# First tokens of a gate-and-mixture kernel: two load queues, means ahead of scales, and another order of the first norms

## The chip, the cores and the metric

The kernel runs on one core of one Trainium2 chip. Its time is the device time of that core in microseconds (us): the median of four runs, 842.18 us (841.93 to 842.66). Beside these there is one profiled execution, whose trace is read below.

## The reference, cut to what matters

Tokens x are 4096 rows of 1024 numbers. Each row is normed, the normed rows feed a gate and a three-layer expert path, and the result is added to x.

```python
xn = (x - mean(x, -1)) / sqrt(var(x, -1) + 1e-5)
g  = sigmoid(xn @ gate_w.T + gate_b)          # product "g"
u_g = xn * g                                  # then a recurrence over tokens and its mean
h  = silu(xn @ w1.T)                          # product "u"
h  = silu(h @ w3.T)                           # product "m"
h  = h @ w2.T
route = top2(softmax(xn @ wr.T))              # expert numbers 0..7 and their gates
out[expert] += gate * h                       # rows 0..7 of the expert output
result = x + recurrence(u_g) * silu(out)
```

Only rows 0 to 7 of the expert output are ever written, so the large products are summed over tokens by expert, and all other rows of the result are rows of x.

## The kernel before, in words

**Tiling.** The tokens are worked off in four super-blocks (`sb`) of 1024. In each the normed tokens stand transposed, as four blocks `xn[sb, I, J]` of 128 partitions x 2048 numbers: I is the half of the tokens, J the half of the channels. A block has four parts of 128x512; `part(block, a)` takes the two that hold token quarter (I, a), as four slices of 256 tokens. The products u (w1), g (gate_w, in super-block 0 alone) and m (w3) are made by seven products of half-size matrices, twice nested: each `Half` is one of the outer seven, and takes seven or eight steps of `small`, four matmuls of 256 columns each. Sums of weight blocks (`fresh_sums`) and of token blocks (`left_sums`) that this needs are made by GpSimd (POOL) into 128x512 tiles `q`. Product 1 of u and g is "plain": eight steps without such sums.

**The first norm.** In super-block 0, mean and variance come from the tokens as they stand in memory. `load_x0` brings 256 rows; `stats0(I, a, ...)` runs on VectorE (DVE): statistics (`bn`), aggregation (`mv`), a root on ScalarE (`sd`), a correction step (`scales`), and two pairs of diagonals (`dg`) with the means and with the scales. Two matmuls with a matrix of ones, `lag` places later in the order, spread them as rows of 256 over all partitions, in a PSUM tile `bc`. `norm0(I, a, J)` then subtracts the mean row and multiplies by the scale row. The quarters (0,0) and (0,1) have their rows in `bc_00` and in `acc`, (1,0) in `bc_10` and (1,1) in `bc_11`. `bc_11` lies in the pool `ps_sm`, which has one bank; ahead of it, `idle` lay there. Sixteen matmuls into `idle` run at the very start, with operands made on the chip.

**What sets the order.** A list `todo` holds steps with a place; the loop at the end runs the steps of the halves by place and, ahead of each, what is due. The order in which instructions are recorded is the order on each engine's queue; an instruction waits for what it reads and for those who still use what it overwrites. Product 1 of u has the places 0 to 14, that of g 3 to 17, product 2 of u begins at 16, and its left-hand sums at 10. The norms have places: (0,1) at 4.6, and block `xn[0,0,1]` at 4.8 and 5. The first sum of `left_sums` for product 2 reads two parts of `xn[0,0,1]`.

**Loads.** All are issued by SyncE (SP), in the order recorded; a load also waits for the landing of the eighth before it. First come the 256 rows in four quarters, the transposed block in quarters between the two halves of w1's first block, the rows of (0,1), gate_w's first block, and the rest of the transposed block.

Lines that matter: at the end of the kernel `idle`, `load_x0(0, 0, 4)`, `first_weights(...)` and the `at(...)` calls of `stats0` and `norm0`.

Of the kernel before, what the change touches and what calls it, by code (L numbers as in the profile page):

```python
# [10 lines left out]
F32 = mybir.dt.float32  # L11
I32 = mybir.dt.int32
U32 = mybir.dt.uint32
AF = mybir.ActivationFunctionType
ALU = mybir.AluOpType
AX = mybir.AxisListType
P = 128
Q = 256
# [4 lines left out]
def kernel(  # L23
# [50 lines left out]
    H = 512  # L74
# [48 lines left out]
                self.home.append(self.tile)  # L123

    NB, NQ = 20, 18
    IDLE = 16
    blocks = deque(
        const.tile([P, 4, 2 * Q], F32, tag=f"b{i}", name=f"b{i}") for i in range(NB)
    )
# [4 lines left out]
    def block(uses=1):  # L134
        return Held(blocks, uses)

    def quarter(uses=1):
        return Held(quarters, uses)
# [5 lines left out]
    pool.memset(ones, 1.0)  # L144
    eps = const.tile([P, 1], F32, tag="eps", name="eps")
    pool.memset(eps, EPS)

    root = const.tile([P, 1], F32, tag="root", name="root")
    act.activation(root, eps, AF.Sqrt)
# [26 lines left out]
    def at(place, f, *args):  # L176

        seq[0] += 1
        heapq.heappush(todo, (place, seq[0], f, args))
# [42 lines left out]
    def scales(o, v, sd, w):  # L222

        r0 = sp.tile([P, w], F32, tag=f"r{w}", name="r0")
        dve.reciprocal(r0, sd)
        e = sp.tile([P, w], F32, tag=f"e{w}", name="e")
        dve.scalar_tensor_tensor(e, r0, -0.5, r0, ALU.mult, ALU.mult)
        dve.tensor_mul(e, e, v)
        dve.scalar_tensor_tensor(o, e, 1.5, r0, ALU.add, ALU.mult)

    def part(t, a):
        return t[:, 2 * a : 2 * a + 2, :].rearrange("p b (k n) -> p (b k) n", n=Q)
# [3 lines left out]
    def stats0(I, a, xb, lag):  # L236

        mv = sp.tile([P, 2, 2], F32, tag="mv", name=f"mv_{I}{a}")
        for tt in range(2):
            xt = xb[:, 2 * tt : 2 * tt + 2, :]  # L240
            bn = sp.tile([P, 2, nc.vector.BN_STATS_DIM], F32, tag=f"bn{tt}", name=f"bn_{I}{a}{tt}")
            for n in range(2):
                dve.bn_stats(bn[:, n, :], xt[:, n, :])
            dve.bn_aggr(mv[:, tt, :], bn)
        xb.drop()
        sd = sp.tile([P, 2], F32, tag="sd2", name=f"sd_{I}{a}")
        act.activation(sd, mv[:, :, 1], AF.Sqrt, bias=eps)
        dg = quarter()

        def diagonals(s, w):  # L250
            for tt in range(2):
                dve.tensor_scalar(
                    dg[:, (2 * s + tt) * P : (2 * s + tt + 1) * P],
                    ident,
                    w[:, tt : tt + 1],
                    None,
                    ALU.mult,
                )

        diagonals(0, mv[:, :, 0])  # L260
        v = sp.tile([P, 2], F32, tag="v2", name=f"v_{I}{a}")
        dve.tensor_scalar(v, mv[:, :, 1], EPS, None, ALU.add)
        rs = sp.tile([P, 2], F32, tag="rs", name=f"rs_{I}{a}")
        scales(rs, v, sd, 2)
        diagonals(1, rs)
        if (I, a) == (1, 1):
            bc = ps_sm.tile([P, 2, Q], F32, tag="sm", name="bc_11")
        elif (I, a) == (1, 0):
            bc = ps_y.tile([P, 2, Q], F32, tag="Y", name="bc_10")
        elif a == 1:  # L270
            bc = acc.rearrange("p (s n) -> p s n", s=2)
        else:
            bc = ps_acc.tile([P, 2, Q], F32, tag="rows", name="bc_00")
        yield lag
        for s in range(2):
            pe.matmul(
                bc[:, s, :],
                ones,
                dg[:, s * Q : (s + 1) * Q],
                start=True,  # L280
                stop=True,
                skip_group_check=True,
            )
        dg.drop()
        bc0[I, a] = bc

    def norm0(I, a, J, parts=1):
        p = part(xn[0, I, J], a)
        bc = bc0[I, a]
        w = 4 // parts  # L290
        for h in range(0, 4, w):
            for s, op in ((0, ALU.subtract), (1, ALU.mult)):
                row = bc[:, s : s + 1, :].to_broadcast([P, w, Q])
                dve.tensor_tensor(p[:, h : h + w, :], p[:, h : h + w, :], row, op)

    def stats(sb, bcs):

# [158 lines left out]
    T_OF = ((1, 0, None), (3, None, 0), (3, 1, None), (2, None, 1))  # L456
    T_AT = (1, 2, 4, 6)

    def load_w(name, KN, uses, before=()):
        t = block(uses)  # L460
        if not before:
            sync.dma_start(t.tile, weights[name][KN])
        for b, f in enumerate(before):
            f()
            sync.dma_start(t[:, b::2, :], weights[name][KN][:, b::2, :])
        return t

    def t_sum(o, t, s, j):
# [87 lines left out]
        sync.dma_start(o.tile, kept[{"u": "w1", "m": "w3"}[kind], i, j])  # L556
        op_ts[kind, sb, i, j] = o

    def first_weights(kind, name, before=()):

        keep = name == "w1"

        def S(i):
            return start[kind, 0, i]

        b = {}

        def load(key, KN, uses, *before):
            b[key] = load_w(name, KN, uses, *before)

        def one():

            op_t[kind, 0, 1] = b[1]

        def two():
            op_t[kind, 0, 2] = b[2]

        def five():
            yield from sub(pool, b[5], b[5], b[1])
            b[1].drop()  # L580
            op_t[kind, 0, 5] = b[5]
            if keep:
                keep_block(name, 5, b[5])

        def six():
            yield from with_bank(b[6], b[6], b[5])
            b[5].drop()
            op_t[kind, 0, 6] = b[6]
            if keep:
                keep_block(name, 6, b[6])  # L590

        def seven():

            yield from sub(pool, b[7], b[6], b[7])
            b[6].drop()
            op_t[kind, 0, 7] = b[7]
            if keep:
                keep_block(name, 7, b[7])

        def four():  # L600
            yield from with_bank(b[4], b[4], b[6])
            b[6].drop()
            op_t[kind, 0, 4] = b[4]
            if keep:
                keep_block(name, 4, b[4])

        def three():
            op_t[kind, 0, 3] = b[3]

        off = 0 if kind == "u" else 1  # L610
        load(1, (0, 0), 2, before)
        one()
        at(-20 + off, lambda: load(2, (1, 0), 2))
        at(-19, two)
        at(-12 + off, lambda: load(5, (0, 1), 3 + keep))
        at(S(5) - 13, five)
        at(2 + off, lambda: load(6, (1, 1), 4 + keep))
        at(S(6) - 16, six)
        at(S(6) - 3 + off, lambda: load(7, (0, 0), 2 + keep))
        at(S(7) - 12, seven)  # L620
        at(S(6) + 8 + off, lambda: load(4, (1, 0), 2 + keep))
        at(S(4) - 14, four)
        at(S(3) - 14, lambda: load(3, (1, 1), 2))
        at(S(3) - 13, three)
        for i in order["u"][1:]:
            if kind == "g" and i in PLAIN_G:
                at(S(i) - 4, lambda i=i: op_t[kind, 0, i].drop())
                continue
            at(
                S(i) + 2 - (11 if i == 2 else 6),  # L630
                lambda i=i: fresh_sums(kind, i, op_t[kind, 0, i], keep),
            )
# [407 lines left out]
    def load_x0(I, a, n=2):  # L1040
        xb = block()
        row = I * H + a * 2 * P
        w = 2 * D // n
        for h in range(n):
            t, c = h * w // D, h * w % D
            sync.dma_start(
                xb.tile.rearrange("p h d -> p (h d)")[:, h * w : (h + 1) * w],
                x[row + t * P : row + (t + 1) * P, c : c + w],
            )
        x0[I, a] = xb  # L1050
# [12 lines left out]
    USES = {(0, 0): 4, (0, 1): 3, (1, 0): 3, (1, 1): 3}  # L1063
    G = {(0, 0): 2, (0, 1): 2, (1, 0): 1, (1, 1): 2}


    idle = ps_sm.tile([P, P], F32, tag="sm", name="idle")
    for _ in range(IDLE):
        pe.matmul(idle, ones, ident, start=True, stop=True, skip_group_check=True)
    load_x0(0, 0, 4)  # L1070
    first = block(USES[0, 0] + G[0, 0])
    xn[0, 0, 0] = first
    first_weights(
        "u",
        "w1",
        [
            lambda b=b: sync.dma_start(first[:, b, :], xT[0, 0, 0, :, b, :])
            for b in range(2)
        ],
    )  # L1080
    load_x0(0, 1)
    first_weights("g", "gw")
    sync.dma_start(first[:, 2:4, :], xT[0, 0, 0, :, 2:4, :])
    at(-27, load_x0, 1, 0)
    at(-26, load_x0, 1, 1)
    at(-25, load_xn, 0, 0, 1, USES[0, 1] + G[0, 1])
    at(-16, load_xn, 0, 1, 0, USES[1, 0] + G[1, 0])
    at(-15, load_xn, 0, 1, 1, USES[1, 1] + G[1, 1])
    at(-10, lambda: stats0(0, 0, x0[0, 0], 0))
    at(-9, norm0, 0, 0, 0, 2)  # L1090
    at(-8, lambda: stats0(0, 1, x0[0, 1], 12.5))
    at(-7, lambda: stats0(1, 0, x0[1, 0], 14))
    at(4.6, norm0, 0, 1, 0)
    at(4.7, lambda: stats0(1, 1, x0[1, 1], 7.5))
    at(4.8, norm0, 0, 0, 1)
    at(5, norm0, 0, 1, 1)
    at(8, norm0, 1, 0, 0)
    at(11, norm0, 1, 0, 1)
    at(15, norm0, 1, 1, 0)
    at(18, norm0, 1, 1, 1)  # L1100
    at(26, consts)
    for IJ in HB:
        at(0, lambda IJ=IJ: left.__setitem__(("u", 0, IJ), xn[(0,) + IJ]))
# [276 lines left out]
```

## Time and profile before

| | us |
|---|---|
| median of four runs | 842.18 (841.93 to 842.66) |
| the profiled execution | 843.08 |
| its span, first to last instruction | 841.3 |
| TensorE matmuls (PE) | 829.0, 99% of the span |
| VectorE (DVE) | 546.3, 65% |
| GpSimd (POOL) | 490.2, 58% |
| ScalarE (ACT) | 243.2, 29% |
| mean granted clock of TensorE | 0.997 of full |

The share of an engine is an average over the whole span. The change touches the first 45 us of it, so the rows of those microseconds count. In a row of the timeline stand the start, the duration, the engine, the operation, output and inputs with their shapes, the number of instructions merged (x), and in brackets the idle time ahead of it with what ended it. The profile counts two records to one matmul of 32-bit numbers. All rows have the line of the helper that records them (L89), so they are told apart by the tiles: `b` is a block, `q` a quarter, `bc` and `acc` hold spread rows, `X_u` is a PSUM tile of product u.

### The profile page before, as it was taken

Reading aid. Unit: us, or ns where it says so; the run is one execution under the profiler, and the core shown is the slowest. Engines: PE = TensorE matmul, PEld = TensorE weight load, DVE = VectorE, ACT = ScalarE, POOL = GpSimd, SP = SyncE. Lnnn points to the kernel's source line nnn. Section 1 sums busy time; section 2 is a strip of 40 time slices with the busy share of each in tenths; the row PEclk is TensorE's granted clock in tenths of the full one; section 3 lists DMA queues with packets and bytes.
Section 4 is the critical chain, followed back from the end, with each engine's and each line's share of the span. In section 5 each row is a group of like instructions: output and inputs, shape, how many; then the busy total and the mean of one; then the engine's idle time right before and its main releaser. Section 6 shows DMA issues by size and latency. Waiting matters only on the chain.

```text
span 841.3 us, 11288 instructions
## 1 busy us (share of the span) xinstructions
PE 829.0 (99%) x4119; PEld 701.6 (83%) x4119; DVE 546.3 (65%) x890; ACT 243.2 (29%) x391; POOL 490.2 (58%) x377
## 2 busy tenths in 40 slices
PE   7999999999999999999999999999999999999997
PEld 6887888888888868888888778888888688888884
DVE  6965699888579427675897225675993246645643
ACT  0214205866121207343012226531122021220112
POOL 0379888785878758546346753753548444474400
PEclk9999999999999999999999999999999999999999
DMA  9935428622995979728966757649774546545700
GB/s 339 422 146 221 155 89 311 226 113 70 396 395 190 317 269 364 287 87 321 407 222 245 269 179 271 237 164 400 284 265 167 184 164 236 201 160 198 282 13 2
DMA packets 55679, 194.97 MB, mean 232 GB/s; under 512 B 6356, under 2 KB 9668, under 8 KB 43592
## 3 DMA queue, kind: packets, MB, share of 16 engines
q1 hardware_dynamic: 55592, 194.24, 62.3%
q8 instruction: 33, 0.54, 0.3%
q14 instruction: 22, 0.18, 0.1%
q10 hardware_dynamic: 32, 0.02, 0.0%
HBM read 171.10 MB, written 39.87 MB: 251 GB/s over the span
## 4 chain that ended last, share of the span: by engine, by line
PE 92%; DMA 3%; DVE 2%; POOL 1%; issue 1%; SPq 0%; ACT 0%; POOLq 0%; DVEq 0%
PE X_u L89 23%; PE X_m L89 20%; PE Z_u L89 12%; PE Z_m L89 11%; PE Y_u L89 6%; PE X_g L89 6%; PE Y_m L89 5%; PE Z_g L89 4%; PE acc L89 2%; PE plT L89 2%; DMA b<-in_w 2%; DVE b L89 1%; DMA w<-q 1%; POOL q L89 1%; PE Y_g L89 1%
## 5 line engine op out<-in xcount | busy, mean ns | idle before, releaser
L89 POOL TENSOR_TENSOR q<-b 128x512 f32<-128x512 f32 x144 | 198.2, 1389 | 230.4 <-DVE b L89 52.7
L89 ACT ACTIVATE b<-b 128x512 f32<-128x512 f32 (+1 forms) x152 | 105.0, 696 | 315.8 <-DVE b L89 311.4
L89 DVE TENSOR_TENSOR b<-b,b 128x512 f32<-128x512 f32 x160 | 155.3, 988 | 2.9
L89 POOL TENSOR_TENSOR q<-b,q 128x512 f32<-128x512 f32 x91 | 130.0, 1432 | 8.8 <-issue 6.7
L89 POOL TENSOR_TENSOR b<-b,b 128x512 f32<-128x512 f32 x72 | 94.8, 1342 | 35.9 <-PE X_u L89 26.4
L89 DVE TENSOR_TENSOR b<-X_u,b 128x512 f32<-128x512 f32 x87 | 59.9, 689 | 72.4 <-PE X_u L89 71.5
L89 PE MATMUL X_u<-q,q 128*128 128x256 f32 x432 | 103.0, 381 | 0.0
L89 DVE TENSOR_TENSOR b<-X_m,b 128x512 f32<-128x512 f32 x84 | 57.4, 687 | 63.7 <-PE X_m L89 63.4
L89 PE MATMUL X_m<-q,q 128*128 128x256 f32 x416 | 98.5, 380 | 0.0
L89 PEld LDWEIGHTS X_u<-q,q 128*128 128x128 f32 x432 | 81.3, 190 | 14.9 <-POOL q L89 1.7
L89 POOL TENSOR_TENSOR q<-q,b 128x512 f32<-128x512 f32 x53 | 71.9, 1357 | 34.5 <-PE X_u L89 28.9
L89 PEld LDWEIGHTS X_m<-q,q 128*128 128x128 f32 x416 | 78.8, 190 | 11.8 <-issue 0.8
L89 DVE TENSOR_TENSOR b<-b,bc 128x1024 f32<-128x1024 f32 (+1 forms) x62 | 72.8, 1178 | 6.2 <-ACT bc L89 5.2
L89 PE MATMUL X_m<-b,b 128*128 128x256 f32 x272 | 63.8, 380 | 0.9 <-POOL b L89 0.9
L89 PE MATMUL X_u<-b,b 128*128 128x256 f32 x248 | 60.4, 388 | 2.8 <-DVE b L89 2.5
L89 PEld LDWEIGHTS X_m<-b,b 128*128 128x128 f32 x272 | 51.3, 190 | 8.6 <-POOL b L89 1.2
L89 PEld LDWEIGHTS X_u<-b,b 128*128 128x128 f32 x248 | 48.0, 195 | 10.7 <-DVE b L89 3.3
L89 PE MATMUL X_u<-b,q 128*128 128x256 f32 x216 | 51.3, 380 | 0.0
L89 PE MATMUL Z_u<-q,b 128*128 128x256 f32 x216 | 51.3, 380 | 0.0
L89 PE MATMUL Y_u<-b,b 128*128 128x256 f32 x216 | 51.3, 380 | 0.0
L89 PE MATMUL Z_u<-q,q 128*128 128x256 f32 x216 | 51.0, 379 | 0.0
L89 DVE TENSOR_TENSOR b<-Z_m,b 128x512 f32<-128x512 f32 x48 | 32.8, 685 | 28.0 <-PE Z_m L89 27.7
(156 smaller groups left out, 1165.2 us busy)
## 6 DMA issues: line engine op xcount, KB each, us to landing
q<-w SPq DMA_DIRECT2D x168, 256.0 KB, 3.2
b<-in_w SPq DMA_DIRECT2D x37, 1024.0 KB, 5.7
b<-w_T SPq DMA_DIRECT2D x25, 1024.0 KB, 5.1
b<-in_xT SPq DMA_DIRECT2D x15, 1024.0 KB, 13.2
w<-q SPq DMA_DIRECT2D x56, 256.0 KB, 6.9
b<-in_x SPq DMA_DIRECT2D x12, 1024.0 KB, 6.0
w_T<-b SPq DMA_DIRECT2D x8, 1024.0 KB, 4.1
b<-in_gw SPq DMA_DIRECT2D x7, 1024.0 KB, 5.7
```

What stands on the lines that cost most here:

```text
L89: r = f(*args, **kwargs)
```

## The change

The first 256 rows (quarter (0,0)) are loaded in four quarters by two queues, SyncE and ScalarE. Their statistics, norm and rows have a function of their own, `first_tokens`: both tiles are aggregated after all statistics; mean and scale rows have a PSUM tile each, `mean_00` in `ps_acc` and `scale_00` in `ps_sm`; two idle matmuls stand behind the mean's matmul and three behind the scale's; the norm of the first block goes by two slices for the mean, one and one for the scale, then two and two. Fourteen idle matmuls instead of sixteen stand at the start, and `idle` moves to `ps_y`. gate_w's first block is loaded in halves, the first of them ahead of w1's second half, both ahead of the rows of (0,1).

The steps after that have other places: the statistics of (1,0) follow the norm of (0,1), those of (1,1) follow them; the norm of `xn[0,0,1]` comes at 11 for its second token quarter and at 12 for its first, so that the first left-hand sum of product 2 (place 10), `q_107` in the order of instructions, stands ahead of it and reads the block as it was loaded. The rows of (1,0) are spread four steps of products later, those of (1,1) one step later.

```diff
-    IDLE = 16
+    IDLE = 14
+    x_first = block()
+    for n in range(2):
+        for t, queue in ((0, sync), (1, act)):
+            queue.dma_start(
+                x_first[:, 2 * t + n, :], x[t * P : (t + 1) * P, n * H : (n + 1) * H]
+            )
...
-        elif a == 1:
+        else:
             bc = acc.rearrange("p (s n) -> p s n", s=2)
-        else:
-            bc = ps_acc.tile([P, 2, Q], F32, tag="rows", name="bc_00")
...
+    def warm(n):
+        for _ in range(n):
+            pe.matmul(idle, ones, ident, start=True, stop=True, skip_group_check=True)
+
+    def first_tokens():
+        ...
+        for n in range(2):
+            for t in range(2):
+                dve.bn_stats(bn[t][:, n, :], x_first[:, 2 * t + n, :])
+        for t in range(2):
+            dve.bn_aggr(mv[:, t, :], bn[t])
+        x_first.drop()
+        sd = sp.tile([P, 2], F32, tag="sd2", name="sd_00")
+        act.activation(sd, mv[:, :, 1], AF.Sqrt, bias=eps)
+        dg = quarter()
+        rows = [
+            ps_acc.tile([P, Q], F32, tag="rows", name="mean_00"),
+            ps_sm.tile([P, Q], F32, tag="sm", name="scale_00"),
+        ]
+        bc0[0, 0] = rows
+        def spread(s, w):
+            ...
+            pe.matmul(rows[s], ones, d, start=True, stop=True, skip_group_check=True)
+        spread(0, mv[:, :, 0])
+        warm(2)
+        ...
+        scales(rs, v, sd, 2)
+        spread(1, rs)
+        dg.drop()
+        warm(3)
+        p = part(xn[0, 0, 0], 0)
+        ...
+        on(0, 2, 0, ALU.subtract)
+        on(0, 1, 1, ALU.mult)
+        on(1, 2, 1, ALU.mult)
+        on(2, 4, 0, ALU.subtract)
+        on(2, 4, 1, ALU.mult)
...
-    idle = ps_sm.tile([P, P], F32, tag="sm", name="idle")
-    for _ in range(IDLE):
-        pe.matmul(idle, ones, ident, start=True, stop=True, skip_group_check=True)
-    load_x0(0, 0, 4)
+    idle = ps_y.tile([P, P], F32, tag="Y", name="idle")
+    warm(IDLE)
     first = block(USES[0, 0] + G[0, 0])
...
+    sync.dma_start(first[:, 0, :], xT[0, 0, 0, :, 0, :])
+    first_half("w1", 0)
+    sync.dma_start(first[:, 1, :], xT[0, 0, 0, :, 1, :])
+    first_half("gw", 0)
+    first_half("w1", 1)
     load_x0(0, 1)
-    first_weights("g", "gw")
+    first_half("gw", 1)
     sync.dma_start(first[:, 2:4, :], xT[0, 0, 0, :, 2:4, :])
...
-    at(-10, lambda: stats0(0, 0, x0[0, 0], 0))
-    at(-9, norm0, 0, 0, 0, 2)
-    at(-8, lambda: stats0(0, 1, x0[0, 1], 12.5))
-    at(-7, lambda: stats0(1, 0, x0[1, 0], 14))
-    at(4.6, norm0, 0, 1, 0)
-    at(4.7, lambda: stats0(1, 1, x0[1, 1], 7.5))
-    at(4.8, norm0, 0, 0, 1)
-    at(5, norm0, 0, 1, 1)
-    at(8, norm0, 1, 0, 0)
-    at(11, norm0, 1, 0, 1)
-    at(15, norm0, 1, 1, 0)
-    at(18, norm0, 1, 1, 1)
+    at(-10, first_tokens)
+    at(-8, lambda: stats0(0, 1, x0[0, 1], 12.4))
+    at(4.6, lambda: stats0(1, 0, x0[1, 0], 5.800000000000001))
+    at(4.5, norm0, 0, 1, 0)
+    at(8, lambda: stats0(1, 1, x0[1, 1], 6))
+    at(12, norm0, 0, 0, 1)
+    at(11, norm0, 0, 1, 1)
+    at(13, norm0, 1, 0, 0)
+    at(15, norm0, 1, 0, 1)
+    at(16, norm0, 1, 1, 0)
+    at(19, norm0, 1, 1, 1)
```

More of the change, by code (lines that the diff above doesn't have):

```diff
@@ L284, in stats0, with norm0 @@
         dg.drop()
-        bc0[I, a] = bc
-    def norm0(I, a, J, parts=1):
+        bc0[I, a] = [bc[:, s, :] for s in range(2)]
+    def norm0(I, a, J):
         p = part(xn[0, I, J], a)
[L289 to L294, printed above, removed]
+        for s, op in ((0, ALU.subtract), (1, ALU.mult)):
+            row = bc0[I, a][s].unsqueeze(1).to_broadcast([P, 4, Q])
+            dve.tensor_tensor(p, p, row, op)
@@ new lines, in warm, with on @@
+    def warm(n):
+        for _ in range(n):
+            pe.matmul(idle, ones, ident, start=True, stop=True, skip_group_check=True)
+    def first_tokens():
+        mv = sp.tile([P, 2, 2], F32, tag="mv", name="mv_00")
+        bn = [
+            sp.tile([P, 2, nc.vector.BN_STATS_DIM], F32, tag=f"bn{t}", name=f"bn_00{t}")
+            for t in range(2)
+        ]
[11 more added lines that the diff above has]
+            ps_sm.tile([P, Q], F32, tag="sm", name="scale_00"),
+        ]
+        bc0[0, 0] = rows
+        def spread(s, w):
+            d = dg[:, s * Q : (s + 1) * Q]
+            for t in range(2):
+                dve.tensor_scalar(
+                    d[:, t * P : (t + 1) * P], ident, w[:, t : t + 1], None, ALU.mult
+                )
+            pe.matmul(rows[s], ones, d, start=True, stop=True, skip_group_check=True)
+        spread(0, mv[:, :, 0])
+        warm(2)
+        v = sp.tile([P, 2], F32, tag="v2", name="v_00")
+        dve.tensor_scalar(v, mv[:, :, 1], EPS, None, ALU.add)
+        rs = sp.tile([P, 2], F32, tag="rs", name="rs_00")
+        scales(rs, v, sd, 2)
[3 more added lines that the diff above has]
+        p = part(xn[0, 0, 0], 0)
+        def on(lo, hi, s, op):
+            row = rows[s].unsqueeze(1).to_broadcast([P, hi - lo, Q])
+            dve.tensor_tensor(p[:, lo:hi, :], p[:, lo:hi, :], row, op)
+        on(0, 2, 0, ALU.subtract)
[3 more added lines that the diff above has]
+        on(2, 4, 1, ALU.mult)
@@ L457, with load_w @@
     T_AT = (1, 2, 4, 6)
-    def load_w(name, KN, uses, before=()):
+    def load_w(name, KN, uses):
         t = block(uses)
[L461 to L465, printed above, removed]
+        sync.dma_start(t.tile, weights[name][KN])
         return t
@@ L557, in load_kept_sum, with first_weights @@
         op_ts[kind, sb, i, j] = o
-    def first_weights(kind, name, before=()):
+    def first_weights(kind, name, b1):
         keep = name == "w1"
@@ L564, in S, with load @@
             return start[kind, 0, i]
-        b = {}
-        def load(key, KN, uses, *before):
-            b[key] = load_w(name, KN, uses, *before)
+        b = {1: b1}
+        def load(key, KN, uses):
+            b[key] = load_w(name, KN, uses)
         def one():
@@ L610, in first_weights @@
         off = 0 if kind == "u" else 1
-        load(1, (0, 0), 2, before)
         one()
@@ L1064, with first_half @@
     G = {(0, 0): 2, (0, 1): 2, (1, 0): 1, (1, 1): 2}
-    idle = ps_sm.tile([P, P], F32, tag="sm", name="idle")
-    for _ in range(IDLE):
-        pe.matmul(idle, ones, ident, start=True, stop=True, skip_group_check=True)
-    load_x0(0, 0, 4)
+    idle = ps_y.tile([P, P], F32, tag="Y", name="idle")
+    warm(IDLE)
     first = block(USES[0, 0] + G[0, 0])
     xn[0, 0, 0] = first
[L1073 to L1080, printed above, removed]
+    first_b = {"w1": block(2), "gw": block(2)}
+    def first_half(name, b):
+        sync.dma_start(first_b[name][:, b::2, :], weights[name][0, 0][:, b::2, :])
+    sync.dma_start(first[:, 0, :], xT[0, 0, 0, :, 0, :])
[3 more added lines that the diff above has]
+    first_half("w1", 1)
     load_x0(0, 1)
-    first_weights("g", "gw")
+    first_half("gw", 1)
     sync.dma_start(first[:, 2:4, :], xT[0, 0, 0, :, 2:4, :])
+    first_weights("u", "w1", first_b["w1"])
+    first_weights("g", "gw", first_b["gw"])
     at(-27, load_x0, 1, 0)
```

## The prediction, made before the changed kernel ran

> **What bounds the kernel now.** I read the page first: which engine is full.
>
> ```profile
> PE 829.0 (99%) x4119; PEld 701.6 (83%) x4119; DVE 546.3 (65%) x890; ACT 243.2 (29%) x391; POOL 490.2 (58%) x377
> ```
>
> TensorE is full once it has begun, so only time in which it has not begun, waits, or runs slowly can be won. The chain of waits, from 0 to 40 us, in order of time, shows the front:
>
> ```profile
> 2.13 5.05 DMA b<-in_x
> ...
> 9.83 0.71 PE bc L89 x2
> 10.54 0.02 issue
> 10.57 0.70 DVE b L89
> 11.27 0.02 issue
> 11.29 0.70 DVE b L89
> 11.99 0.04 issue
> 12.03 5.41 PE X_u L89 x16
> 17.44 1.73 PE X_g L89 x8
> ```
>
> The first product waits until 12.03 for the last quarter of tokens (landed 7.18), the scale row (9.83) and two passes of the norm (10.57, 11.29). Then 16 matmul records take 5.41 us, where 8 take 1.73 later. The stretches by microsecond say why (stretch, its length, busy time of each engine, then the granted clock):
>
> ```profile
> 12.00:13.00 1.00, 0.97 (x4) 0.89 (x5) 0.97 (x2) 0.00 (x0) 0.00 (x0) 0.89 1.05 434
> 13.00:14.00 1.00, 1.00 (x3) 0.79 (x3) 1.00 (x3) 0.00 (x0) 0.00 (x0) 0.50 1.04 438
> ```
>
> The clock fell to 0.50 at about 12.8; the stretch from 16 to 17 has 0.90, so it came back at 16.2. Last, the timeline from 25 to 75 us, where VectorE, not TensorE, has to be watched:
>
> ```profile
> 28.30 1.27 POOL L89 TENSOR_TENSOR q<-b 128x512 f32<-128x512 f32 x1 [26.46 <-DMA b<-in_w]
> ...
> 28.43 1.42 DVE L89 TENSOR_SCALAR q<-ident,mv 128x128 f32<-128x128 f32 x2
> ...
> 29.64 1.33 POOL L89 TENSOR_TENSOR q<-b,q 128x512 f32<-128x512 f32 x1
> 29.76 1.23 DVE L89 TENSOR_SCALAR v<-mv 128x2 f32<-128x2 f32 x1
> ...
> 32.08 2.47 DVE L89 TENSOR_TENSOR b<-b,bc 128x1024 f32<-128x1024 f32 x2
> ...
> 36.27 1.03 PE L89 MATMUL bc<-q,ones 128*128 128x256 f32 x4
> ...
> 42.31 1.89 PE L89 MATMUL X_u<-b,b 128*128 128x256 f32 x8
> ```
>
> VectorE works without a break here; beside GpSimd's two sums its diagonals took 1.42 us (0.43 elsewhere, at 8.06) and a 128x2 operation 1.23 us (0.16 at 8.41). The row of 36.27 spreads token quarter (1,1); it waits for nothing. The row of 42.31 is my finish line: product 2 of u. Behind it each engine's order is the same in both programs, so a gain or loss at this line is one at the end.
>
> **The change part by part.**
>
> *Two queues.* SyncE's first issues are 0.46 us apart, so xT's moves from 2.60 to 1.66: at most 0.94 earlier. But the mean busy share of the DMA engines is 0.95 to 1.05 from 2.25 to 3.25 us with one queue, so little is free: at worst 0. I take 0.3, nearer the full engines. The page "DMA: Bandwidth & Descriptors", section "Issuing engines are not separate DMA queues", says a second issuer saves only issue time on the sequencer; by that alone the term would be up to 0.94 and the total 843.3. ScalarE's two issues stand ahead of its table load (1.28) and hide in its 5.95 us of idle before 8.18; uncovered they would cost 0.92.
>
> *First tokens.* The aggregation of the first tile used to lie in a wait (5.07); now both follow the last statistics: +0.12 (7.94 to 8.06). The scale matmul moves from 9.83 to 9.83 - 0.30 + 0.12 = 9.65. The subtraction has its own PSUM tile and runs beside it (0.72 from start to start); then a quarter pass, estimated from 128x512 at 0.69 as 0.36, and 0.07 of hand-over: first product at 9.65 + 1.15 = 10.80, not 12.03. The quarters that follow (0.36, 0.72, 0.69) end at 12.5, when the second half-product (1.73 after 10.80) wants them.
>
> *Idle matmuls.* Their records are 0.21 us apart at first, 0.11 later, two to each. Two (0.44) fit in the 1.28 us between mean and scale; three (0.67) end at 9.65 + 0.43 + 0.67 = 10.75, just in time (at the slow rate 0.2 to 0.3 late). With them no long break is left at the front, so I take the half clock as gone: X_u's 16 records took 17.27 - 12.03 = 5.24 instead of 3.45. X_g would start at 10.80 + 3.45 = 14.25 instead of 17.27: 3.0 us gained so far.
>
> *gate_w's half.* Whole, it landed by 16.1 (the issue at 16.11 waits for it); X_g at 14.25 would wait 1.9. The half takes the place of w1's second half, whose landing let go the issue at 11.07: now 10.8, in time. w1's second half lands by 12.0, needed at 16.0. Both nothing.
>
> *Next late: tokens (0,1).* They land 0.52 MB later; the landings at 12.31 and 13.58 show 1.27 us for that. So 13.58 + 1.27 - 0.30 = 14.55, and from there 3.18 to the last diagonal (14.65 to 17.83): 17.75. TensorE comes to their rows at 14.25 + 3.45 = 17.70: 0.15 lost, uncertain by 0.3. VectorE has gained nothing: 17.8 before, 17.8 now.
>
> *The new order.* VectorE: norm of (0,1), first block, 18.9 to 21.4 (it waits for the rows matmul, 1.03); statistics (1,0), 4.53 as before, to 25.95; statistics (1,1), 2.84 to its diagonals: 28.8. Before, the norm of (0,1) filled 23.2 to 25.6 and statistics (1,1) began at 25.59; the order changes but the sum hardly does. GpSimd: its sums start when w1's second block lands, 28.30 - 0.2 = 28.1. The third, q_107, adds two quarters of block xn[0,0,1]; before, it followed that block's norm (37.02). Now it stands ahead, takes the block as it lands, and the norm waits for it. So three sums run in a row, to 28.1 + 4.05 = 32.15. VectorE's diagonals and v pass between them; the rest of the chain (from 31.10 to 32.08 before, 0.98) comes after: norm of xn[0,0,1] from 33.15. If only the last diagonals are held: 32.65; if more is held, 34.0.
>
> *The new wait.* scale_00 has taken the PSUM bank that the rows of (1,1) need. It is read last by the multiplication of norm0(0,0,1), the fourth of that block's passes; so this rows matmul now waits for it on TensorE, with Z_u, Z_g and product 2 queued behind. Four passes took 4.86 (32.08, and 2.47 more from 34.47, to 36.94): the matmul can start at 33.15 + 4.90 = 38.05. TensorE comes to it 24.15 us of matmuls after the first product (14 groups of 1.725): 10.80 + 24.15 + 0.15 = 35.10. It stands for 2.95 us. From there 0.86 + 2 x 1.725 = 4.31 lead to product 2: 42.36, against 42.31. The whole front is given back, whatever the front gained.
>
> *The clock again.* In the trace the half clock lasted 3.4 us, from 12.8 to 16.2; in the 3.4 us before it TensorE had worked about 1.2 (records at 9.83 and from 12.03), 35%; in the 3.4 before those about 1.7 (idle matmuls to 7.3 and the mean's), 50%, and no drop followed. A stand of 2.95 leaves 14% of such a stretch if it lies in one. If the stretches do not keep step with the kernel and 40% is the bound, it drops in about 6 of 10 placements (2.05 must fall in one: (3.41 - 2.95 + 2 x 0.90) / 3.41); on this trace's grid the stand would straddle an edge at 36.7 and nothing drops. The cost is half of 3.42: 1.71.
>
> The page "TensorE: Matmul & The Clock Gate", section "Why this matters for your kernels", warns of idle gaps over some 3 us. By that a stand of 2.95 keeps the clock, and the time would be the rival's 842.2. But the row speaks against it: the clock fell at 12.8 with no gap over 1.9 us.
>
> **Sum.** The profiled execution took 843.08 (span 841.3, 1.78 around it), 0.90 over the median of 842.18; I apply the difference to the median. +0.05 + 1.71 = +1.76: 843.08 becomes 844.84, the median 843.9.
>
> **The rivals.** (a) The clock holds: +0.05, so 842.2, from 840.9 (queues 0.94, only the last diagonals held) to 843.4 (no gain by the queues, more held). For it: the straddling grid. It decides if the stand is under 2 us or split. (b) The wait hardly binds, because VectorE is through with xn[0,0,1] by 35.1: then the 3.0 less 0.15 stays and it is 839.3, faster. Its place is the rows of (1,1); it needs norms from 30.2, before q_107 is done (32.15), so I find little for it; a much earlier landing could do it in part. (c) More of statistics (1,1) is held by the sums: norms from 34.0, +0.85 and the clock drops: 844.8.
>
> **How the numbers follow.** Forecast 0.55, its own range 842.9 to 844.9 (0.40 of it over 843.9, 0.15 under); (a) 0.25; (b) 0.10; (c) 0.10. A measurement here can tell about 0.2% (1.7 us) from no change. Slower 0.40 + 0.10 = 0.50; same 0.15 + 0.25 = 0.40; faster 0.10. The range takes in (a) and (c) with their bounds and leaves out (b): 841.0 to 845.0.
>
> **What would show it.** Right: first X_u at 10.8, clock 1.00 from 9 to 17, three GpSimd sums in a row from 28.1, TensorE idle from 35 to 38 ahead of bc, released by VectorE, then 0.50 for 3.4 us. Wrong: no idle time ahead of that bc; clock 1.00 behind it (rival a); first X_u after 11.5 (queues or quarters bring nothing, and only the stand gets shorter).

## The result and the profile after

The changed kernel takes 843.89 us (median of 34 executions), the kernel before 842.43 in the 56 runs beside it: ratio 1.0020, 95% interval 1.0014 to 1.0026. It is slower by about a fifth of a per cent, and 843.9 had been forecast. The profiled execution took 845.04 us (span 843.3) against 843.08 (841.3).

The page's first lines say that TensorE is as full as before; the 2 us cannot be seen there:

```profile
PE 829.6 (98%) x4125; PEld 703.3 (83%) x4125; DVE 546.7 (65%) x891; ACT 242.8 (29%) x391; POOL 489.9 (58%) x377
```

The timeline shows the front (start, busy time, engine, operation; in brackets the idle time before it and what ended it):

```profile
7.69 0.70 PE L89 MATMUL mean<-q,ones 128*128 128x256 f32 x2 [1.08 <-DVE q L89]
...
8.94 0.70 PE L89 MATMUL scale<-q,ones 128*128 128x256 f32 x2
...
10.16 3.72 PE L89 MATMUL X_u<-b,b 128*128 128x256 f32 x16
...
13.45 1.29 DVE L89 BATCH_NORM_STATS2 bn<-b 128x6 f32<-128x512 f32 x2 [1.70 <-DMA b<-in_x]
13.71 1.89 PE L89 MATMUL X_g<-b,b 128*128 128x256 f32 x8
...
18.13 0.70 PE L89 MATMUL acc<-q,ones 128*128 128x256 f32 x2 [0.37 <-DVE q L89]
```

In the kernel before, X_g's row is this:

```profile
17.27 1.89 PE L89 MATMUL X_g<-b,b 128*128 128x256 f32 x8
```

X_g starts at 13.71 instead of 17.27: the front is 3.56 us ahead. The same timeline further on, from GpSimd's third sum (`q<-b`) to product 2:

```profile
31.08 1.27 POOL L89 TENSOR_TENSOR q<-b 128x512 f32<-128x512 f32 x1
31.24 1.12 DVE L89 SCALAR_TENSOR_TENSOR e<-r 128x2 f32<-128x2 f32 x1
...
33.19 2.47 DVE L89 TENSOR_TENSOR b<-b,acc 128x1024 f32<-128x1024 f32 x2
...
35.57 1.21 DVE L89 TENSOR_TENSOR b<-b,mean 128x1024 f32<-128x1024 f32 x1
36.82 1.22 DVE L89 TENSOR_TENSOR b<-b,scale 128x1024 f32<-128x1024 f32 x1
...
38.10 1.13 PE L89 MATMUL bc<-q,ones 128*128 128x256 f32 x4 [2.87 <-DVE b L89]
...
39.06 3.54 PE L89 MATMUL Z_u<-b,b 128*128 128x256 f32 x8
...
44.20 1.89 PE L89 MATMUL X_u<-b,b 128*128 128x256 f32 x8
```

The rows of (1,1), at 38.10, wait 2.87 us for "b", which is the pass over `scale` that ended just before; the eight records of Z_u then take 3.54 us instead of 1.89. This idle time of TensorE ahead of the rows of (1,1) is called the stand below. Product 2, the finish line, starts at 44.20, 1.89 later than before, and the profiled time grew by 1.96. The stretches by microsecond (after the length, busy share and count for PE, PEld, DVE, ACT, POOL; then granted clock, DMA share, GB/s) show the clock in each of these places:

```profile
12.00:13.00 1.00, 1.00 (x6) 0.90 (x5) 0.00 (x0) 0.00 (x0) 0.00 (x0) 1.00 1.04 422
13.00:14.00 1.00, 1.00 (x7) 0.87 (x6) 0.55 (x1) 0.00 (x0) 0.00 (x0) 1.00 1.00 391
...
36.00:37.00 1.00, 0.00 (x0) 0.00 (x0) 0.97 (x2) 0.00 (x0) 0.00 (x0) 1.00 1.02 426
...
40.00:41.00 1.00, 1.00 (x4) 0.82 (x3) 1.00 (x2) 0.00 (x0) 1.00 (x2) 0.50 1.04 434
```

From 12 to 14 us, where the clock of the kernel before fell (0.89, then 0.50), it is now full; after the stand it is 0.50. A stretch at half the clock is called a fall below.

### The profile page after: what moved, and what is told of

Same layout as the page of the kernel before. It is cut to its first block, busy times and chain, and to the rows that moved or that the text cites. A ratio compares the mean times of both kernels' runs of the same rounds, so it can differ in the third digit from the quotient of the medians.

```text
span 843.3 us, 11302 instructions
## 1 busy us (share of the span) xinstructions
PE 829.6 (98%) x4125; PEld 703.3 (83%) x4125; DVE 546.7 (65%) x891; ACT 242.8 (29%) x391; POOL 489.9 (58%) x377
## 4 chain that ended last, share of the span: by engine, by line
PE 89%; DMA 4%; DVE 4%; POOL 1%; issue 1%; SPq 0%; ACT 0%; POOLq 0%; DVEq 0%
PE X_u L89 22%; PE X_m L89 20%; PE Z_u L89 11%; PE Z_m L89 11%; PE Y_u L89 6%; PE X_g L89 5%; PE Y_m L89 5%; PE Z_g L89 3%; DVE b L89 2%; PE plT L89 2%; PE acc L89 2%; DMA b<-in_w 2%; DMA b<-in_x 1%; DMA w<-q 1%; POOL q L89 1%
## 5 line engine op out<-in xcount | busy, mean ns | idle before, releaser
L89 PEld LDWEIGHTS X_u<-q,q 128*128 128x128 f32 x432 | 81.4, 190 | 14.7 <-POOL q L89 1.7
L89 DVE TENSOR_TENSOR b<-b,bc 128x1024 f32<-128x1024 f32 x56 | 67.7, 1212 | 7.4 <-ACT bc L89 5.8
L89 PE MATMUL X_u<-b,b 128*128 128x256 f32 x248 | 58.7, 381 | 1.3 <-DVE b L89 1.0
L89 DVE TENSOR_TENSOR b<-Z_u,b 128x512 f32<-128x512 f32 x47 | 32.3, 688 | 30.3 <-PE Z_u L89 29.7
```

What stands on the lines that cost most here:

```text
L89: r = f(*args, **kwargs)
```

## The experiments

Each row is the median of an experiment beside that of the kernel before on the same chip and in the same rounds, with the ratio and its interval. The last column counts the executions whose mean granted clock was 0.997 or less (for the changed kernel out of two executions more than the median has, one of them the profiled one): one half-clock stretch of 3.4 us in 840 lowers the mean by 0.002. This mean tells neither where the clock fell nor how often (0.995 would be two such stretches, an estimate from the same figures), so the column is a count of executions with a fall somewhere, and near its edge an uncertain one.

| kernel | us | before | ratio | clock at most 0.997 |
|---|---|---|---|---|
| the changed kernel | 843.89 | 842.43 | 1.0020 (1.0014 to 1.0026) | 19 of 36 |
| e1_one_bank | 840.47 | 842.58 | 0.9972 (0.9961 to 0.9982) | 0 of 8 |
| e2_idle_in_stand | 843.31 | 842.58 | 1.0010 (1.0002 to 1.0019) | 0 of 12 |
| e3_one_queue | 844.13 | 842.58 | 1.0024 (1.0011 to 1.0037) | 6 of 12 |
| e4_norm_swap | 840.75 | 842.58 | 0.9977 (0.9967 to 0.9986) | 0 of 9 |
| e5_norms_before_sum | 840.06 | 842.90 | 0.9958 (0.9946 to 0.9971) | 0 of 6 |
| e6_e5_one_queue | 840.88 | 842.90 | 0.9977 (0.9964 to 0.9990) | 1 of 8 |
| e7_e5_no_idle | 840.24 | 842.90 | 0.9959 (0.9946 to 0.9972) | 0 of 6 |
| e8_e5_gate_later | 840.44 | 842.90 | 0.9965 (0.9952 to 0.9978) | 0 of 5 |
| e9_old_order | 841.46 | 842.41 | 0.9987 (0.9978 to 0.9996) | 0 of 11 |
| e10_short_stand | 843.45 | 842.41 | 1.0014 (1.0004 to 1.0024) | 3 of 11 |
| e11_e5_tokens_sooner | 839.43 | 842.41 | 0.9961 (0.9948 to 0.9975) | 0 of 5 |

**The stand taken away: another bank.**

```diff
-            ps_acc.tile([P, Q], F32, tag="rows", name="mean_00"),
-            ps_sm.tile([P, Q], F32, tag="sm", name="scale_00"),
+        both = ps_acc.tile([P, 2, Q], F32, tag="rows", name="both_00")
+        rows = [both[:, s, :] for s in range(2)]
```

> Mean and scale of the first tokens share one PSUM bank, as two halves, so the rows of (1,1) get a bank that nobody has used. Nothing else is moved. Theory (the rows matmul waits for the bank, 2.87 us, and the stand brings the half clock, 1.75 us): TensorE comes to the rows at 35.2 and goes on at once, clock 1.00 from 9 to 45, product 2 at 44.20 - 2.87 - 1.75 = 39.6, profiled time about 840.4, median 839.2 to 840.6 (the median holds executions in which the clock did not fall). Rival 1 (the front is bound by arrivals and norms anyway, so another wait takes the place of this one): product 2 or a row shortly behind it stands instead, and the median stays within 1 us of 843.9. Rival 2 (the half bank is the price: the subtraction has to wait for the scale matmul): first product 0.4 to 0.7 us later than 10.16, the rest as in the theory.

The timeline of this kernel, TensorE and VectorE:

```profile
9.88 2.79 DVE L89 TENSOR_TENSOR b<-b,both 128x512 f32<-128x512 f32 x5 [0.79 <-PE both L89]
...
11.08 3.72 PE L89 MATMUL X_u<-b,b 128*128 128x256 f32 x16 [0.57 <-DVE b L89]
...
35.43 1.03 PE L89 MATMUL bc<-q,ones 128*128 128x256 f32 x4
...
39.75 1.89 PE L89 MATMUL X_u<-b,b 128*128 128x256 f32 x8
```

The rows have no bracket: TensorE doesn't wait. Product 2 comes 4.45 us sooner (2.87 + 1.75 = 4.62 expected), the profiled time is 840.46, and the median is 3.42 below the changed kernel's. Of the three, the theory holds, and so does rival 2: the subtraction now waits for the scale's matmul. The first product is 0.92 us later, of which 0.21 stood ahead of it already (the mean's matmul starts at 7.90 for 7.69), so this wait costs 0.71, the upper end of the 0.4 to 0.7 given. By the last product ahead of the rows of (1,1) only 0.36 of the 0.92 is left (it starts at 33.70 for 33.34), since TensorE loses less at the rows of (0,1).

**The stand taken away: the order of two norms.**

```diff
-    at(12, norm0, 0, 0, 1)
+    at(10.9, norm0, 0, 0, 1)
     at(11, norm0, 0, 1, 1)
```

> Only the order of two norms on VectorE is changed: the block half whose last pass sets free the bank (2.43 us for two passes) goes ahead of the other half. Theory: the bank comes free 2.4 us sooner, at 35.65, the stand shrinks from 2.87 to about 0.45, the clock stays at 1.00, product 2 at 44.20 - 2.42 - 1.75 = 40.0, profiled time 840.9, median 839.8 to 841.1. Rival 1 (another wait takes its place, since the other half is normed 2.4 us later): median 842.5 to 844. Rival 2 (the stand is not due to this bank): it stays at 2.87, median 843.9.

```profile
34.60 1.22 DVE L89 TENSOR_TENSOR b<-b,scale 128x1024 f32<-128x1024 f32 x1
...
36.06 1.03 PE L89 MATMUL bc<-q,ones 128*128 128x256 f32 x4
...
40.38 1.89 PE L89 MATMUL X_u<-b,b 128*128 128x256 f32 x8
```

The last read of the bank now ends at 35.82, ahead of the matmul at 36.06, which doesn't wait. In this execution tokens (0,1) came a microsecond later (their statistics from 14.45 instead of 13.45), so TensorE itself was later; even so the profiled time was 840.96 and the median 840.75, both inside what was expected. Two kernels that touch different things, a bank and an order, give the same 3 us: it is this wait, with the fall behind it.

**The clock by itself: idle matmuls in the stand.** Both kernels keep the wait. Their idle matmuls are written over the first half of a product that lies in the bank of Z_u, so that part of the output is not what the reference computes.

```diff
         yield lag
+        if (I, a) == (1, 1):
+            for _ in range(12):        # 4 in the other kernel
+                pe.matmul(halves[0].Z[:, 0:P], ones, ident, start=True, stop=True, ...)
         for s in range(2):
```

> The wait stays; ahead of the waiting rows matmul TensorE is given 12 idle matmuls, 0.22 us each, 2.6 us in all, which lie in the stand of 2.87 us. Theory (the stand itself makes the clock fall): the rows matmul still starts at 38.1, the clock stays at 1.00 behind it, product 2 at 44.20 - 1.75 = 42.45, and the profiled time is about 843.3, the median 842.3 to 843.0. Rival (the fall is due to something else, such as the low load over a longer time or the transfers at that time): 0.50 for 3.4 us behind the rows as before, median 843.9 or, if the idle matmuls overrun the stand, up to 0.5 more.

> The changed kernel with 4 idle matmuls, 0.9 us, ahead of the waiting rows matmul, so that TensorE stands for about 1.95 us instead of 2.87. Like the kernel with 12, it overwrites half a product's bank with them, so part of the output is changed. Theory (the fall needs a stand of over 2 us): the clock stays, mean clock 0.998 or more in at least 10 of 12 executions, median 842.9 to 843.4. Rival (any stand of some 2 us can bring it, as in the kernel before, where it fell with no gap over 1.9): mean clock 0.997 or less in a third or more of the executions, median 843.6 to 844.2.

With twelve, the timeline:

```profile
35.15 2.84 PE L89 MATMUL Z_u<-ident,ones 128*128 128x128 f32 x24
38.17 1.13 PE L89 MATMUL bc<-q,ones 128*128 128x256 f32 x4 [0.18 <-DVE b L89]
39.14 1.89 PE L89 MATMUL Z_u<-b,b 128*128 128x256 f32 x8
```

The rows start where they did, and Z_u takes 1.89 again. Product 2 is 1.61 earlier (42.59), the profiled time is 843.28, and none of 12 executions counts as one with a fall. The median, 843.31, is only 0.58 below the changed kernel's, 0.3 above the band given: the half clock is there in about half of the changed kernel's executions, not in all. Its 19 with the lower clock have a median of 845.14, the 7 at 0.998 of 843.36, the 10 at 0.999 and above of 843.05. The wait alone, without a fall, is about the 2.84 us between the median of this kernel and that of e1.

With four, TensorE stood for 2.01 us ahead of the rows, and the profiled execution kept its clock:

```profile
38.01 1.13 PE L89 MATMUL bc<-q,ones 128*128 128x256 f32 x4 [2.01 <-DVE b L89]
38.97 1.89 PE L89 MATMUL Z_u<-b,b 128*128 128x256 f32 x8
```

The lower clock came in 3 of 11: more falls than the theory allows ("at least 10 of 12" without), fewer than the rival's third. Stands of 0.18, 2.01 and 2.87 us go with 0 of 12, 3 of 11 and 19 of 36 executions. The first and the last of these differ clearly; 3 of 11 is too few to be told from either, and each stand was measured in one execution only, so that an edge near 2 us is neither shown nor excluded.

**One queue, with the stand and without.**

```diff
-        for t, queue in ((0, sync), (1, act)):
+        for t, queue in ((0, sync), (1, sync)):
```

> All four quarters of the first tokens are issued by SyncE, as before the change; all else as in the changed kernel. Theory (the queues bring about 1 us at the first product, and the stand takes it back): first product 0.9 to 1.1 us later, at 11.1 to 11.3, TensorE comes to the rows of (1,1) 0.5 to 1.0 us later, the stand shrinks to about 2.0 to 2.4 and ends where it did, at 38.1. With the clock falling all the same the median stays at 843.9; with a stand of 2 us the clock may hold more often, which would give 842.5 to 843.5. Rival (what is gained at the front reaches the end): median 844.7 to 845.0.

> As e5_norms_before_sum, but all four quarters of the first tokens are issued by SyncE. Theory (the second queue brings 1.0 to 1.36 us at the first product, of which most is lost again at the rows of (0,1), where TensorE waits for VectorE): first product at about 11.5, the rows of (0,1) 0.3 to 0.6 us later, median 0.2 to 0.6 above that kernel. Rival (all of the gain reaches the end): 1.0 to 1.4 above it.

The timeline of the kernel with the stand:

```profile
38.80 1.13 PE L89 MATMUL bc<-q,ones 128*128 128x256 f32 x4 [2.77 <-DVE b L89]
39.77 1.89 PE L89 MATMUL Z_u<-b,b 128*128 128x256 f32 x8
...
43.23 1.89 PE L89 MATMUL X_u<-b,b 128*128 128x256 f32 x8
```

With the stand, the first product was at 11.52, 1.36 later than in the changed kernel, outside the expected 0.9 to 1.1. The theory had the stand shrink and end where it did; it was 2.77 us and ended at 38.80 rather than 38.1, because the later tokens moved VectorE's whole chain by 0.7. This much does reach product 2: in this execution, which had no fall, it starts at 43.23, 0.64 after that of the kernel with twelve idle matmuls, which had none either. Half of the executions still have the lower clock, five of these six at 0.995, and the median, 844.13, can't be told from 843.89. Without the stand, the first product was 0.99 later (11.35 for 10.36), product 2 was 0.63 later (40.02 for 39.39), and the median 0.82 higher, between the two expectations (the intervals of the two ratios overlap, so the 0.63 of the traces is the firmer figure). One of its eight executions has the lower clock (0.994), though the profile shows no stand at the rows of (1,1): a fall can come elsewhere too. The second queue is worth 1.0 to 1.4 at the front and about 0.6 to 0.8 at the end.

**The norms ahead of GpSimd's sum.** In the changed kernel q_107 adds its two quarters as they land, before their norm; here it takes the normed quarters again, as in the kernel before.

```diff
-    at(12, norm0, 0, 0, 1)
-    at(11, norm0, 0, 1, 1)
+    at(9.8, norm0, 0, 0, 1)
+    at(9.9, norm0, 0, 1, 1)
```

> Both norms of block xn[0,0,1] go ahead of GpSimd's sum q_107 in the program, the half that frees the bank first; the banks are those of the changed kernel. Theory: GpSimd's third sum (31.08 to 32.35) no longer stands ahead of the norms, so the 128x2 operation that took 1.12 us takes 0.16, norms start at about 32.2 instead of 33.2, the bank is free at 34.6, TensorE comes to the rows of (1,1) at 34.9 to 35.9 and doesn't stand; clock 1.00; product 2 at 39.3 to 40.2; median 839.7 to 840.9. Rival (GpSimd, whose sums now wait for the second norm, to about 37, becomes late for product 2): a stand of 1 us or more behind product 2's start, median 841.5 or more.

```profile
31.32 0.16 DVE L89 SCALAR_TENSOR_TENSOR e<-r 128x2 f32<-128x2 f32 x1
...
32.31 1.21 DVE L89 TENSOR_TENSOR b<-b,mean 128x1024 f32<-128x1024 f32 x1
...
33.55 1.22 DVE L89 TENSOR_TENSOR b<-b,scale 128x1024 f32<-128x1024 f32 x1
...
35.07 1.03 PE L89 MATMUL bc<-q,ones 128*128 128x256 f32 x4
...
39.39 1.89 PE L89 MATMUL X_u<-b,b 128*128 128x256 f32 x8
```

The norms start at 32.31, 0.88 before those of the changed kernel, in which GpSimd's third sum stands ahead. GpSimd's q_107 now starts at 37.24, and nobody waits for it. Median 840.06. Two orders are changed at once here, that of the norms against the sum and that of the two norms; the 0.88 belongs to the first.

**The idle matmuls at the front, and gate_w.** Both start from the kernel above: one drops `warm(2)` and `warm(3)`, the other moves one line.

```diff
-    first_half("gw", 0)
     first_half("w1", 1)
     load_x0(0, 1)
+    first_half("gw", 0)
     first_half("gw", 1)
```

> As e5_norms_before_sum, but without the five idle matmuls between the mean's and the scale's rows and the first product. Theory (they hold the clock): 0.50 for 3.4 us from about 12 to 13 in the profiled execution or in part of the executions, which costs 1.7 less what TensorE waits for the rows of (0,1), 0.4 to 0.8: 1.0 to 1.4 where it falls, median 0.3 to 1.2 above that kernel, mean clock lower by 0.002 in those executions. Rival (the clock holds without them, the first product's earlier start is enough): the same median within 0.2.

> As e5_norms_before_sum, but the first half of gate_w is issued behind tokens (0,1), just ahead of its second half, as the whole was before. Theory (gate_w's first half sooner is what lets X_g follow): X_g waits until about 16 instead of starting at 13.7, 2.3 us, of which the wait at the rows of (0,1), 0.4 to 0.8, goes, since those tokens land 1.2 us sooner: 1.3 to 1.9 above that kernel, 1.7 more where the clock falls in that stand. Rival (tokens (0,1), which land sooner, are the bound): the same or up to 0.5 less.

Without the five idle matmuls TensorE waits for the mean's diagonals (1.36) and, as the timeline says, twice more ahead of the first product:

```profile
9.10 0.70 PE L89 MATMUL scale<-q,ones 128*128 128x256 f32 x2 [0.55 <-DVE q L89]
...
10.31 3.72 PE L89 MATMUL X_u<-b,b 128*128 128x256 f32 x16 [0.52 <-DVE b L89]
```

None of the six executions counts as one with a fall, and the median is the same within 0.2: the theory is wrong, the rival holds. Six executions cannot exclude a rare fall, but it isn't the half of them that the kernel before shows (0.997 or less in 31 of 62). It isn't these idle matmuls that took the fall away at the front; that the shorter wait did (0.52 instead of 1.50 ahead of the first product) was only argued.

With gate_w's half later:

```profile
14.61 1.99 PE L89 MATMUL X_g<-b,b 128*128 128x256 f32 x8 [0.55 <-DMA b<-in_gw]
```

X_g waited 0.55 and not 2.3, and at the end 0.38 remains, far under the 1.3 to 1.9 expected. The first tile of tokens (0,1) landed by 11.94 instead of 13.46, and TensorE no longer waits for their rows: most of what one transfer loses, the other returns.

**The other statistics and norms in the order of before**, in the changed kernel.

```diff
-    at(4.6, lambda: stats0(1, 0, x0[1, 0], 5.800000000000001))
-    at(4.5, norm0, 0, 1, 0)
-    at(8, lambda: stats0(1, 1, x0[1, 1], 6))
...
+    at(-7, lambda: stats0(1, 0, x0[1, 0], 14))
+    at(4.6, norm0, 0, 1, 0)
+    at(4.7, lambda: stats0(1, 1, x0[1, 1], 7.5))
...
```

> The changed kernel with its new front, but statistics and norms of the other tokens in the order they had before the change (statistics (1,0) ahead of the norm of (0,1); norms of xn[0,0,1] ahead of q_107, the half that frees the bank first). Theory A (the late norms and the bank are all that gives the front back, and the rest of the new order is worth little): no stand ahead of the rows of (1,1), median 839.8 to 840.8. Theory B (the new order is needed, since TensorE now comes to the second half of the first tokens' block at about 23 and its norm would end at 25 to 25.6): a stand of 1.5 to 2.6 us there, released by VectorE, median 841.5 to 843.5, more if the clock falls in it.

```profile
23.45 0.70 PE L89 MATMUL bc<-q,ones 128*128 128x256 f32 x2 [0.58 <-DVE q L89]
```

There was no stand at (1,1), so theory A is right in that part; but TensorE stood 0.58 at the rows of (1,0), as VectorE waited for those tokens until 18.78. Product 2 came at 40.74, 1.35 behind the 39.39 of e5, and the median, 841.46, is at the lower edge of theory B's band; but the stand is neither at the place nor of the size that it gave. Part of the new order is therefore worth having; by this wait it is the statistics (1,0) behind the norm of (0,1), which no run changes alone. The late norms of xn[0,0,1] are what cost.

**Tokens (0,1) ahead of w1's second half**, from e5.

```diff
-    first_half("w1", 1)
     load_x0(0, 1)
+    first_half("w1", 1)
```

> As e5_norms_before_sum, but tokens (0,1) are issued ahead of w1's second half, 0.5 MB sooner. Theory (what is left of the front's gain is lost at the rows of (0,1)): the tokens land at about 12.2 instead of 13.46, TensorE doesn't wait for their diagonals, product 2 starts at 39.0 instead of 39.39, median 839.4 to 839.9. Rival (w1's second half is now late): a wait of TensorE for it at about 15.6, median 840.3 to 841.5.

```profile
17.23 1.03 PE L89 MATMUL acc<-q,ones 128*128 128x256 f32 x4
...
38.81 1.89 PE L89 MATMUL X_u<-b,b 128*128 128x256 f32 x8
```

The statistics of (0,1) run from 11.73, their rows don't wait, and w1's second half is still in time. Product 2 starts at 38.81, 0.58 before that of e5; the ratio to before (0.9961) can't be told from e5's (0.9958). So the theory holds in the trace, and the time does not show it. These two, e5 and e11, beat both kernels, by about 0.4% on the kernel before.

## Why the prediction was right, step by step

*Two queues: mis-sized.* The term was 0.30, between 0 and 0.94; it is 0.99 to 1.36 at the first product. I took full DMA engines as a sign that little was free. The Trainium skill's page "DMA: Bandwidth & Descriptors", section "Issuing engines are not separate DMA queues", allows the issue time alone, by the estimate up to 0.94; that was nearer, though the runs lie a little above it.

*First tokens and first product.* From scale row to first product 1.15 was worked out, and 1.22 measured (8.94 to 10.16); the first product came 0.64 before the forecast 10.80, all of it from the queues.

*The idle matmuls: a wrong reason with the right effect.* Clock 1.00 from 9 to 17 came, but in e7 it came without them.

*gate_w's half: bound taken for value.* "Landed by 16.1" was read from an issue that waited, an upper bound; in e8, which issues the half that X_g needs first behind tokens (0,1), X_g went on at 14.61.

*Tokens (0,1): the loss mis-sized.* The forecast 14.55 is for their second tile, and it came at about 14.7: SyncE's issue at 14.73 waits for its landing (the wait that ends at 13.45 is for the first tile). That this is near has two errors in it: with one queue (e3, the issue at 15.55) they come 1.9 later than in the kernel before, not 1.27, and two queues take 0.8 of it back, not 0.30. The last diagonals end at 18.07, forecast 17.75, and TensorE was at their rows at 17.17, forecast 17.70, so 0.63 was lost there (18.66 for 18.03) instead of 0.15. This loss takes back most of what the queues brought beyond their 0.30: TensorE was through with the products ahead of the rows of (1,1) at 35.07, counted as in the forecast (33.34 + 1.725), for the forecast 35.10.

*The three sums, the norms and the new wait: right.* Norms from 33.19 (33.15), the matmul at 38.10 (38.05), the stand 3.03 counted from 35.07 (2.95; the bracket's 2.87 counts from the modelled end of the product). Two small errors cancel in it: the sums began at 28.45 instead of 28.1, and they and the rest of the chain took 4.74 instead of 5.05. That the third sum holds VectorE is seen in the 128x2 operation of 31.24, 1.12 us, and 0.16 in e5; it reads two inputs from SBUF. The Trainium skill's page "SBUF — State Buffer", section "Who interferes with whom", says that such an operation contends with a GpSimd instruction that reads SBUF; the row agrees, and e5, where no sum stands beside it, starts its norms 0.88 sooner.

*The clock: right in the profiled execution, over-counted in the median.* The half clock came behind the stand, for 3.4 us; e2 prices it at 1.61 to 1.76 us. The Trainium skill's page "TensorE: Matmul & The Clock Gate", section "Why this matters for your kernels", would have let a stand under 3 us pass; the profile decides against it here for 2.87 us (for 2.01 us there is only the count, 3 of 11, and no profile with a fall). I had put it at 6 in 10 placements of 2.95 us and the runs give 19 of 36. That is no proof of the working: it took 1.2 and 1.7 us of work in the two stretches ahead of the old fall, and the profile's busy time there (9.38 to 12.80 and 5.97 to 9.38) is 1.47 and 2.23, 43% and 65%, by which the same working gives 7 in 10 or more. I then charged the fall whole to a median.

*Why 843.9 was met all the same.* Both profiled executions had one fall, before at the front and after at the stand, so the two cancel in their difference, forecast +1.76 and measured 1.96. In the medians of both kernels about half of the executions have it. Before, the executions with the lower clock have a median of 843.16 and those at 0.999 and above 842.29, 0.87 apart; after, 2.1 apart. The median difference of 1.46 lies between what the two groups give, 0.76 and 1.98. So the mechanism was right, and that the number was met within 0.05 us is luck: the difference was 0.30 smaller than the forecast 1.76, and the kernel before was 0.25 slower than in the four runs that the forecast started from. Why a fall costs the kernel before only half as much was not tried.

*The rivals.* (b), that the wait hardly binds, is what e1, e4, e5 and e11 make true: 839.4 to 840.8 for its 839.3. (a), the clock holds, is e2: 843.3 for its 842.2. Its 0.05 was a difference to an execution with a fall, and it was added to a median in which only half of the executions have one; beside the executions before without a fall (842.29), e2 is 1.0 slower. (c) did not come: the norms started as forecast.

## What to carry to other kernels

When a tile moves to another PSUM buffer, follow that buffer to its next user and ask when the tile's last reader runs; a wait placed on the full engine gives back what was won ahead of it, unless the gain also moves the chain that is waited for (0.64 of 1.36 us in e3), and swapping two norms was worth 3 us of 843. Size a change at the front at the next place where another engine's chain is awaited, not where it is made: of 1.0 to 1.4 us from the second queue, 0.6 to 0.8 arrived. A profile shows one execution; a cost that comes in some executions only enters a median by its share.

## What the runs showed of the hardware

The length of a stand alone does not settle whether the clock falls, as far as one profile of each kernel can tell: it fell behind 2.87 us in the changed kernel's profile, held through 2.77 in that of e3 and through 2.01 in that of e10, and the changed kernel has the lower clock in 19 of 36 executions. Short matmuls laid into the stand, which leave 0.18 us of it, prevented the fall (0 of 12).

VectorE's wait for the first tile of tokens (0,1) ended anywhere from 13.3 to 14.5 us in profiles whose issues up to there are the same (the changed kernel, e4, e5, e10), a scatter of over 1 us. Where TensorE waits for them it reaches product 2: 40.38 in e4 with the latest, 39.39 in e5.
